# The last weights of an item in the attention denominators: summed by VectorE first, or by TensorE directly, in two of sixteen batch elements

## The chip, the cores and the metric

The kernel runs on one core of a Trainium2 chip. The metric is the device time of one execution in microseconds (us). Everything is in fp32.

## The reference, cut to what matters

The input is x of shape (16, 256, 32, 32): 16 batch elements of 256 channels and 1024 tokens. Each element passes two layers. Layer 0 is an attention with 4 heads of width 64 and a residual. Layer 1 is group norm, an attention with 8 heads of width 32 and a residual, group norm, and an MLP of 256 to 1024 to 256 with gelu and a residual. The change touches layer 1's attention alone:

```python
attn = jnp.einsum('bhnd,bhmd->bhnm', q, k) * scale + phys_bias
attn = jax.nn.softmax(attn, axis=-1)
out = jnp.einsum('bhnm,bhmd->bhnd', attn, v)
out = out.transpose(0, 2, 1, 3).reshape(B, H * W, C)
out = out @ proj_w.T + proj_b
```

A softmax needs, for each query, the sum of the exponentials over all 1024 keys. The kernel does not subtract a maximum first; it watches the range of the denominators, and a second, general pass exists for data that leave it.

## The kernel before

**Stages.** The elements are worked on one after the other. For each one, `first_pass` runs `attention_a` (layer 0), `attention_b` (layer 1) and the MLP, overlapped: the MLP pieces of one element and the projections (q, k, v) of the next one are "pieces" that `run` puts between the steps of an attention. In the first element (b = 0) `attention_b` has only its own seven remaining q, k, v pieces, in steps 0 to 6. In the last one (b = 15) it has these and three MLP pieces, in steps 7, 10 and 13; the other four MLP pieces follow after the stage. The elements between have more pieces to fill with, the next element's projections among them.

**One step of `attention_b`.** Its work is cut into four items (t, c): a half of the queries (t, 512 of them) and four of the eight heads (c). Each item is cut into four units of two key blocks (kb = 0, 2, 4, 6, of 128 keys each), so there are 16 units and 16 steps, counted from 0 here. Step n does this, in program order:

1. `scores(u)`: 16 matmuls into PSUM (s_b, L502; the profile has two records for each fp32 matmul), then five exponentials on ScalarE (L517) into four tiles of weights e_b, each 128 x 1024 in fp32. The scores of one unit use all eight PSUM banks: the banks b0 and b1 and three double tiles.
2. `add` of the unit's first weight tile: a VectorE addition (L533) into one of the item's two running sums es_b. In the item's first unit the first two tiles start the sums.
3. `weigh` of the unit before: 8 matmuls of weights and values into acc_b in bank b0 (L554), which are added to the result res_b, on VectorE (L567), or copied by ScalarE in the item's first unit (L565).
4. `add` of the three other weight tiles.
5. A tick of `later`, and the step's piece, if it has one.

**Denominators.** When an item's last unit has been weighed, `normalise` is put off to the tick behind it. It runs four matmuls of 128 x 32 (den_b, L576, in bank b1), one for each head, of the two running sums against columns that hold exp(bias). Then `denominators` has ScalarE copy den_b (L328), sends it through a DMA into another layout (sp_b, L333), and after some ticks inverts it (L337), writes it to DRAM (row_b, L338), reads it back as four broadcasts (rd_b, L343), and after some ticks more VectorE scales the result by it (L601). The two counts are 1 and 1 for the first three items, 3 and 5 for the fourth, except in the last element, where the fourth item's reciprocal is taken on VectorE directly from PSUM (L586) and the scaling follows at once. The scaling of an item with c = 1 schedules the output projection j of its half of the queries one tick later; the one of the fourth item is handed to the next attention in all but the last element.

**Order.** `later` is a list of functions with a count of ticks. The order on each engine is fixed when the program is built: a planner takes the instructions in the order of the program, but may put a ready instruction ahead of one that is still waiting by its own estimates. `tc.keep_in_program_order` holds some VectorE instructions (additions after the first of a unit, the reciprocal, the scaling) to the order written. Weight tiles e_b have 8 buffers, the sums es_b 4, the inverted denominators rd_b one.

Of the kernel before, what the change touches and what calls it, by code (L numbers as in the profile page):

```python
# [235 lines left out]
def first_pass(ctx, tc, x, out, k):  # L236
    nc = tc.nc
    B, C, S = x.shape
    CC, SB, NT = C // P, S // P, S // TB
    HC = k["w1"].shape[2] // P  # L240
    later = Later()
# [25 lines left out]
    def wide(name, n=None):  # L267
        if n is None:
            n = next(m for m in order if m not in kept)
        use(n)  # L270
        return ps_s.tile([P, 2, TB], F32, tag=f"s{n}", name=name)

    def bank(name, n):
        return ps_a.tile([P, TB], F32, tag=f"b{n}", name=name)
# [203 lines left out]
    def attention_b(b, qT, kT, v, project):  # L478
        key, D = f"b_{b}", D1
        G = P // D  # L480


        items = [(NT - 1, 0)]
        items += [(t, 0) for t in range(NT - 1)] + [(t, 1) for t in range(NT)]
        units = [(i, kb) for i in range(len(items)) for kb in range(0, SB, 2)]
        res, sums = {}, {}

        def scores(i, kb):
            t, c = items[i]
            es = []  # L490
            for m in range(2):
                if m == 0:
                    one, two = (bank(f"s_{key}_{i}_{kb}_{n}", n) for n in range(2))
                    tiles = [None, wide(f"s_{key}_{i}_{kb}_1")]
                    outs = [one, two, tiles[1][:, 0, :], tiles[1][:, 1, :]]
                else:
                    tiles = [wide(f"s_{key}_{i}_{kb + 1}_{n}") for n in range(2)]
                    outs = [tiles[g // 2][:, g % 2, :] for g in range(G)]
                for g in range(G):
                    for h in range(0, P, HALF):  # L500
                        k0 = (kb + m) * P + h
                        nc.tensor.matmul(  # L502
                            outs[g][h : h + HALF, :],
                            kT[g * D : (g + 1) * D, c, k0 : k0 + HALF],
                            qT[g * D : (g + 1) * D, c, t * TB : (t + 1) * TB],
                            start=True,
                            stop=True,
                        )
                for n in range(G // 2):
                    e = work.tile(  # L510
                        [P, 2, TB], F32, tag="e", name=f"e_{key}_{i}_{kb + m}_{n}", bufs=8
                    )
                    for to, s in (
                        [(e, tiles[n])] if tiles[n] is not None
                        else [(e[:, 0, :], one), (e[:, 1, :], two)]
                    ):
                        nc.scalar.activation(to, s, AF.Exp, scale=float(D) ** -0.5)  # L517
                    es.append(e)
            return i, kb, es

        def add(i, kb, es, which):
            if kb == 0 and 0 in which:
                sums[i] = [
                    work.tile([P, 2, TB], F32, tag="es", name=f"es_{key}_{i}_{n}", bufs=4)
                    for n in range(G // 2)
                ]
            for n in which:
                if kb == 0 and n < G // 2:  # L530
                    continue
                d = sums[i][n % 2]
                ins = nc.vector.tensor_add(d, es[n % 2] if kb == 0 else d, es[n])  # L533
                if n:
                    tc.keep_in_program_order(ins)

        def result(t):
            if t < NT - 1 and b == 0:  # L540
                return [
                    work.tile([P, TB], F32, tag="g", name=f"res_{key}_{t}_{c}", bufs=16)
                    for c in range(CC)
                ]
            tag = "res1" if t == NT - 1 else "res" if b < B - 1 else "q0"
            r = act.tile([P, CC, S if tag == "q0" else TB], F32, tag=tag, name=f"res_{key}_{t}")
            return [r[:, c, :TB] for c in range(CC)]

        def weigh(i, kb, es):
            t, c = items[i]  # L550
            acc = bank(f"acc_{key}_{i}_{kb}", 0)
            for m in range(2):
                for g in range(G):
                    nc.tensor.matmul(  # L554
                        acc[g * D : (g + 1) * D, :],
                        v[:, kb + m, c * G + g],
                        es[2 * m + g // 2][:, g % 2, :],
                        start=(m == 0),
                        stop=(m == 1),
                    )  # L560
            if t not in res:
                res[t] = result(t)
            r = res[t][c]
            if kb == 0:
                nc.scalar.copy(r, acc)  # L565
            else:
                nc.vector.tensor_add(r, r, acc)  # L567
            if kb == SB - 2:
                later.after(1, lambda: normalise(i, r, i == len(items) - 1))

        def normalise(i, r, last):
            t, c = items[i]
            at_end = last and b == B - 1
            den = bank(f"den_{key}_{i}", 1)
            for g in range(G):
                nc.tensor.matmul(  # L576
                    den[g * D : (g + 1) * D, :],
                    k["eones"][:, c * G + g],
                    sums[i][g // 2][:, g % 2, :],
                    start=True,  # L580
                    stop=True,
                )
            full = work.tile([P, TB], F32, tag="full", name=f"rd_{key}_{i}", bufs=1)
            if at_end:

                nc.vector.reciprocal(full, den)  # L586
                scale(i, r, last, full)
                for tot, what in ((dsum, den), (isum, full)):
                    part = small.tile([P, 1], F32, tag="part", name="part")
                    nc.vector.tensor_reduce(part, what, AX.X, ALU.add)  # L590
                    nc.gpsimd.tensor_add(tot[:, :1], tot[:, :1], part)
                return
            denominators(
                f"{key}_{i}", den, full, full,
                (3, 5) if last else (1, 1),
                lambda full: scale(i, r, last, full),
            )

        def scale(i, r, last, full):
            t, c = items[i]  # L600
            tc.keep_in_program_order(nc.vector.tensor_mul(r, r, full))  # L601
            if c == CC - 1:
                issue = project(t, res[t])
                if last and b + 1 < B:
                    handed.append(issue)
                else:
                    later.after(1, issue)

        cols[0] = D
        pending = None  # L610
        for u in units:
            now = scores(*u)
            add(*now, (0,))
            if not pending:

                yield
                add(*now, (1, 2, 3))
                pending = now
                continue
            weigh(*pending)  # L620
            add(*now, (1, 2, 3))
            pending = now
            yield
        weigh(*pending)
        yield
        cols[0] = P
# [193 lines left out]
    def attention_1(b, qkv_tiles, xb, norm):  # L820
        q, kk, v = qkv_tiles
        stats = small.tile([P, CC, NT, 6], F32, tag="st1", name=f"st1_{b}", bufs=2)

        def project(t, res):
            return out_proj(
                f"j{b}", k["wpj"],
                lambda kc: res[kc],
                k["pjb"], xb, t, stats, (lambda: norm(stats)) if t == NT - 1 else None,
            )

        return attention_b(b, q, kk, v, project)
# [144 lines left out]
    start = first_qk[::2] + first_qk[1::2] + first_v  # L976
# [23 lines left out]
    last = NT * CC * SB // 2 - 1  # L1000
    for b in range(B):
        if b + 1 < B:
# [5 lines left out]
                lambda st, b=b, xn=xn: group_norm(  # L1008
                    f"g{b}", xs[b], st, k["g1w"], k["g1b"], "res", xn, 3
                ),  # L1010
# [39 lines left out]
        for m, pieces in enumerate(rest):  # L1050
# [5 lines left out]
                lambda st, b=b, hn=hn: group_norm(  # L1056
                    f"h{b}", xs[b], st, k["g2w"], k["g2b"], "q1", hn,
                    3 if b + 1 < B else 1,
                ),
# [311 lines left out]
```

## Time and profile before

| | us |
|---|---|
| median of 3 runs | 3708.99 |
| lowest and highest | 3707.59, 3709.53 |
| the profiled execution | 3707.96 |
| its span | 3706.2 |
| TensorE busy in the span | 3685.2 |
| VectorE busy | 2498.0 |
| ScalarE busy | 2084.0 |
| `attention_b` of the first element | 122.65 to 215.49 |
| `attention_b` of the last element | 3528.94 to 3628.14 |

PE is TensorE, PEld its weight loads, DVE VectorE, ACT ScalarE, POOL GpSimd and SP the engine that issues most DMAs. A row of a group gives the line of the kernel, the engine, the operation, the tiles out and in and the count, then busy time, mean nanoseconds of one, and the idle time before it with what ended it. A row in order of time gives its start, its length from the first to the last of its instructions, engine, line, operation and tiles, and in brackets the idle time before and its releaser. A row of waits gives who waited for whom, the total, the number of times and the longest. The granted TensorE clock was 0.999 of full speed over the span.

### The profile page before, as it was taken

The page shows a single profiled execution, that of the slowest core. Times are in us where ns is not written, and L with a number is a line of the kernel's source. Part 1 is how long each engine was busy: PE and PEld are TensorE (multiplying, and loading weights), DVE is VectorE, ACT ScalarE, POOL GpSimd, SP SyncE. Part 2 cuts the span into 40 slices and gives each one's busy share as a digit, 9 for nine tenths or more (in the row PEclk, how much of TensorE's full clock was granted, in tenths as well). Part 3 has the DMA queues.
Part 4 walks back from the last instruction along what each step waited for, and adds up shares of the span by engine and source line. Part 5 has one row for each costly group of instructions (what it writes and reads, how often), then busy time and mean ns, then how long its engine had stood idle before and what let it go on. Part 6 is the DMA issues. An engine that isn't in the chain of part 4 may idle for free.

```text
span 3706.2 us, 79254 instructions
## 1 busy us (share of the span) xinstructions
PE 3685.2 (99%) x34349; PEld 1319.4 (36%) x34349; DVE 2498.0 (67%) x3150; ACT 2084.0 (56%) x2704; POOL 102.9 (3%) x251
## 2 busy tenths in 40 slices
PE   9999999999999999999999999999999999999999
PEld 4333343333423334333343333433333333333333
DVE  4685757757576675766757667586675867657675
ACT  4665646555465564655646465564655656556472
POOL 1000000000000000000000000000000000000000
PEclk9999999999999999999999999999999999999999
DMA  2000100000001010010000100001010000000000
GB/s 87 12 14 10 33 13 13 31 10 33 13 13 36 4 33 13 19 30 7 30 13 19 30 7 31 13 19 30 8 36 7 22 27 13 30 7 22 16 8 27
DMA packets 63395, 77.80 MB, mean 21 GB/s; under 512 B 35038, under 2 KB 37854, under 8 KB 63038
## 3 DMA queue, kind: packets, MB, share of 16 engines
q1 hardware_dynamic: 60892, 71.85, 6.4%
q8 instruction: 271, 4.44, 0.5%
q14 instruction: 86, 0.70, 0.1%
q10 hardware_dynamic: 1746, 0.40, 0.1%
q0 software_dynamic: 400, 0.41, 0.1%
HBM read 54.28 MB, written 17.56 MB: 19 GB/s over the span
## 4 chain that ended last, share of the span: by engine, by line
PE 94%; DVE 3%; issue 2%; ACT 1%; DMA 1%; ACTq 0%; SPq 0%; POOL 0%; DVEq 0%
PE s_b L502 12%; PE acc_b L554 12%; PE s_a L368 12%; PE m L849 12%; PE acc_a L389 11%; PE m L314 10%; PE qk_a L314 6%; PE qk_b L314 5%; PE o L314 3%; PE v_a L314 3%; PE j L314 3%; PE v_b L314 2%; PE den_b L576 1%; DVE es_b L533 1%; PE den_a L420 1%
## 5 line engine op out<-in xcount | busy, mean ns | idle before, releaser
L517 ACT ACTIVATE e_b<-s_b 128x1024 f32<-128x1024 f32 (+1 forms) x1280 | 982.7, 865 | 151.0 <-PE s_b L502 151.0
L533 DVE TENSOR_TENSOR es_b<-es_b,e_b 128x1024 f32<-128x1024 f32 x768 | 899.5, 1219 | 217.2 <-ACT e_b L517 217.1
L376 ACT ACTIVATE e_a<-s_a 128x1024 f32<-128x1024 f32 x512 | 520.8, 1024 | 360.4 <-PE s_a L368 348.1
L502 PE MATMUL s_b<-q,k 32*64 32x512 f32 x8192 | 527.2, 601 | 9.8 <-DVE v L768 7.1
L368 PE MATMUL s_a<-q,k 64*64 64x512 f32 x4096 | 532.6, 593 | 1.1
L389 PE MATMUL acc_a<-e_a,v 64*64 64x512 f32 x4096 | 528.5, 589 | 0.0
L401 DVE TENSOR_TENSOR es_a<-es_a,e_a 128x1024 f32<-128x1024 f32 x384 | 469.4, 1222 | 75.9 <-ACT e_a L376 60.4
L554 PE MATMUL acc_b<-e_b,v 128*32 128x512 f32 x4096 | 492.1, 598 | 0.0
L849 PE MATMUL m<-gn_h,w 128*128 128x512 f32 x1024 | 452.9, 596 | 0.4 <-DVE gn_h L723 0.4
L314 PE MATMUL m<-g,w2s 128*32 128x512 f32 (+1 forms) x3320 | 404.2, 592 | 0.0
L857 ACT ACTIVATE g<-m,m1b 128x512 f32<-128x512 f32 x256 | 175.9, 687 | 339.3 <-PE m L849 339.3
L866 DVE TENSOR_TENSOR g<-g,g 128x512 f32<-128x512 f32 x320 | 209.3, 686 | 147.7 <-ACT g L857 147.4
L502 PEld LDWEIGHTS s_b<-q,k 32*64 32x64 f32 x8192 | 166.3, 130 | 337.3 <-issue 124.6
L849 PEld LDWEIGHTS m<-gn_h,w 128*128 128x128 f32 x1024 | 191.0, 190 | 236.7 <-issue 235.2
L389 PEld LDWEIGHTS acc_a<-e_a,v 64*64 64x64 f32 x4096 | 161.9, 133 | 277.5 <-issue 235.8
L368 PEld LDWEIGHTS s_a<-q,k 64*64 64x64 f32 x4096 | 152.6, 133 | 278.1 <-issue 207.9
L554 PEld LDWEIGHTS acc_b<-e_b,v 128*32 128x32 f32 x4096 | 108.5, 109 | 357.5 <-ACT e_b L517 194.7
L314 PE MATMUL qk_a<-x,wp 128*32 128x512 f32 (+1 forms) x1856 | 233.7, 592 | 0.4 <-ACT k L747 0.4
L314 PE MATMUL qk_b<-gn_g,wq 128*32 128x512 f32 (+1 forms) x1280 | 234.0, 592 | 0.0
L567 DVE TENSOR_TENSOR res_b<-res_b,acc_b 128x512 f32<-128x512 f32 x192 | 131.8, 687 | 143.7 <-PE acc_b L554 143.7
L314 PEld LDWEIGHTS m<-g,w2s 128*32 128x32 f32 (+1 forms) x3320 | 121.5, 112 | 262.2 <-issue 235.8
L768 DVE TENSOR_TENSOR v<-v_b,eones 128x512 f32<-128x512 f32 x64 | 44.1, 689 | 166.0 <-PE v_b L314 166.0
(131 smaller groups left out, 2371.8 us busy)
## 6 DMA issues: line engine op xcount, KB each, us to landing
d_a<-row_a SPq DMA_DIRECT2D x64, 256.0 KB
rd_b<-row_b SPq DMA_DIRECT2D x252, 64.0 KB
out_dram<-x SPq DMA_DIRECT2D x63, 256.0 KB
x<-in_x_dram SPq DMA_DIRECT2D x30, 512.0 KB
x<-in_x_dram SPq DMA_DIRECT2D x4, 256.0 KB
w<-in_L_conv_mlp_w_dram SPq DMA_DIRECT2D x1, 1024.0 KB
w2s<-in_L_conv_mlp_w_dram SPq DMA_DIRECT2D x4, 256.0 KB
sp_b<-rd_b SPq DMA_DIRECT2D x63, 8.0 KB
```

The source lines that it names most:

```text
L314: nc.tensor.matmul(o[sl], w[:, sl], r, **flags)
L368: nc.tensor.matmul(s[h : h + HALF, g, :], kT[g * D : (g + 1) * D, c, kb * P + h : kb * P + h + HALF], qT[g * D : (g + 1) * D, c, t * TB : ...
L376: nc.scalar.activation(e, s, AF.Exp, scale=float(D) ** -0.5)
L389: nc.tensor.matmul(accs[i][h][g * D : (g + 1) * D, :], v[h * HALF : (h + 1) * HALF, kb, c * 2 + g], e[h * HALF : (h + 1) * HALF, g, :], st ...
L401: nc.vector.tensor_add(sums[i], held[i] if kb == 1 else sums[i], e)
L502: nc.tensor.matmul(outs[g][h : h + HALF, :], kT[g * D : (g + 1) * D, c, k0 : k0 + HALF], qT[g * D : (g + 1) * D, c, t * TB : (t + 1) * TB] ...
L517: nc.scalar.activation(to, s, AF.Exp, scale=float(D) ** -0.5)
L533: ins = nc.vector.tensor_add(d, es[n % 2] if kb == 0 else d, es[n])
L554: nc.tensor.matmul(acc[g * D : (g + 1) * D, :], v[:, kb + m, c * G + g], es[2 * m + g // 2][:, g % 2, :], start=(m == 0), stop=(m == 1),)
L849: nc.tensor.matmul(ps, k["w1"][:, cc, hc * P : (hc + 1) * P], hn[0][:, cc, t * TB : (t + 1) * TB], start=(cc == 0), stop=(cc == CC - 1),)
L857: nc.scalar.activation(g, ps, AF.Gelu, bias=k["m1b"][:, hc : hc + 1])
L866: (nc.vector.tensor_add if plus else nc.vector.tensor_sub)(d, d, gs[(*what, i)])
```

## The change

In `attention_b` of the first and the last element, the four weight tiles of an item's last unit are no longer added to the running sums. The denominators' matmuls take the two sums and these four tiles, in three accumulated rounds of four matmuls in place of one round. In these elements `normalise` is also called at once in `weigh`, behind the last unit's weighted sums, and not from the tick behind that step; what it schedules with counts of ticks then counts from there. The other fourteen elements keep the old form.

```diff
+        direct = b in (0, B - 1)
...
         def add(i, kb, es, which):
+            if direct and kb == SB - 2:
+                return
...
             if kb == SB - 2:
-                later.after(1, lambda: normalise(i, r, i == len(items) - 1))
-
-        def normalise(i, r, last):
+                last = i == len(items) - 1
+                if direct:
+                    normalise(i, r, last, sums[i] + es)
+                else:
+                    later.after(1, lambda: normalise(i, r, last, sums[i]))
+
+        def normalise(i, r, last, parts):
             t, c = items[i]
             at_end = last and b == B - 1
             den = bank(f"den_{key}_{i}", 1)
-            for g in range(G):
-                nc.tensor.matmul(
-                    den[g * D : (g + 1) * D, :],
-                    k["eones"][:, c * G + g],
-                    sums[i][g // 2][:, g % 2, :],
-                    start=True,
-                    stop=True,
-                )
+            for m in range(0, len(parts), G // 2):
+                for g in range(G):
+                    nc.tensor.matmul(
+                        den[g * D : (g + 1) * D, :],
+                        k["eones"][:, c * G + g],
+                        parts[m + g // 2][:, g % 2, :],
+                        start=(m == 0),
+                        stop=(m + G // 2 == len(parts)),
+                    )
```

Here G is 4 (heads of an item), D is 32, SB is 8 (key blocks) and B is 16.

## The prediction

> **What bounds the kernel now.** I read the page first (share of each engine, then the chain that ended last), then the two stretches that the diff touches, the second attention of the first and of the last element, by their busy time, their waits and the rows in order of time.
>
> ```profile
> span 3706.2 us, 79254 instructions
> ...
> PE 3685.2 (99%) x34349; PEld 1319.4 (36%) x34349; DVE 2498.0 (67%) x3150; ACT 2084.0 (56%) x2704; POOL 102.9 (3%) x251
> ...
> PE 94%; DVE 3%; issue 2%; ACT 1%; DMA 1%; ACTq 0%; SPq 0%; POOL 0%; DVEq 0%
> ...
> L533 DVE TENSOR_TENSOR es_b<-es_b,e_b 128x1024 f32<-128x1024 f32 x768 | 899.5, 1219 | 217.2 <-ACT e_b L517 217.1
> ```
>
> TensorE carries 94% of the chain, so a microsecond of new PE work anywhere counts unless PE would have stood idle there. Busy time of the two stretches (first row: first element; second: last):
>
> ```profile
> 122.65:215.49 92.84, 90.16 (x994) 26.30 (x993) 77.56 (x79) 67.39 (x91) 3.02 (x6) 1.00 0.04 11
> 3528.94:3628.14 99.20, 96.73 (x1089) 29.06 (x1088) 85.74 (x93) 69.51 (x95) 2.09 (x6) 1.00 0.05 13
> ```
>
> Columns: length, then PE, PEld, DVE, ACT, POOL. PE looks 97% busy, but matmuls overlap, so I counted records at the spacing at which groups follow each other. A group of 16 acc_b records takes 1.74 us before the next one starts (149.08 to 150.82), 8 den_b records 0.86:
>
> ```profile
> 150.82 1.04 PE L576 MATMUL den_b<-es_b,eones 128*32 128x512 f32 x8
> ...
> 151.68 1.90 PE L314 MATMUL qk_b<-gn_g,wq 128*32 128x512 f32 x16
> ```
>
> The first element has 16 units of 3.44 us (32 s_b, 16 acc_b), 7 pieces of 1.72, four denominators of 0.86 and one j of 3.43: 73.9 us of work in 92.8. PE really idles 19 us there, and by the same count 15 us in the last element. DVE idles 15 and 13. So which idle is DVE's fault? Waits in the first stretch:
>
> ```profile
> PEld s_b L502 <- DVE res_b L567: 7.5, 8, 1.8
> DVE res_b L567 <- PE acc_b L554: 7.3, 8, 1.9
> ```
>
> PE waits for the L567 addition, which frees bank 0, but DVE has mostly been waiting for PE first. The loop is: scores, acc, addition, next scores; its 0.69 us addition is the idle, not DVE's load. Steps 7 to 12 (a step is one unit) show both kinds:
>
> ```profile
> 171.28 1.92 PE L554 MATMUL acc_b<-e_b,v 128*32 128x512 f32 x16
> 173.02 1.04 PE L576 MATMUL den_b<-es_b,eones 128*32 128x512 f32 x8
> 173.27 0.69 DVE L567 TENSOR_TENSOR res_b<-res_b,acc_b 128x512 f32<-128x512 f32 x1 [0.54 <-PE acc_b L554]
> 174.01 2.82 PE L502 MATMUL s_b<-q,k 32*64 32x512 f32 x32
> 174.18 0.63 ACT L328 COPY rd_b<-den_b 128x512 f32<-128x512 f32 x1
> ...
> 186.40 1.92 PE L554 MATMUL acc_b<-e_b,v 128*32 128x512 f32 x16
> ...
> 188.37 1.22 DVE L533 TENSOR_TENSOR es_b<-es_b,e_b 128x1024 f32<-128x1024 f32 x1
> 189.50 0.68 DVE L567 TENSOR_TENSOR res_b<-res_b,acc_b 128x512 f32<-128x512 f32 x1
> ```
>
> At 173 us the den_b group already covers the addition (scores at 174.01, 0.13 us after it). At 189.50 DVE is late: acc_b ended at 188.32, and an addition of the kind to be removed stood in front.
>
> [...]
>
> **The change, part by part.**
> (a) Added: each item's denominator gets three rounds of four matmuls for one. Two extra rounds are 16 records, 1.72 us at 0.86 per 8; eight items (four in each of two elements) make 13.8 us. They stand right behind acc_b, before the next scores. The only idle there is 0.13 us where no piece follows, since the first round and the addition fill it; with a piece behind it, none. All 13.8 is on the path (bounds 12 to 14).
> (b) Removed: four additions an item, 32 in all, 37 us of DVE. Only what PE loses to DVE comes back. First element: step 7 (L567 at 168.64, acc_b over at 168.30) 0.3; step 11 1.2; the last den_b, which waits for the sums, takes 1.41 instead of 1.04, 0.4. Together 1.9. Last element: step 8 (den_b over at 3582.46, scores at 3583.29) 0.7; step 14 0.2; last den_b 0.4. Together 1.3. After it, from 3628.14 to 3647.24, PE has 40 full records of 0.43 us and little else, 17.5 us in 19.1; freed of the additions DVE reaches the reciprocal (L586, 3630.12) sooner relative to den_b, and I take 1.1 of the 1.6 (bounds 0.5 and 1.6). Sum of (b): 4.3 (bounds 3 and 6).
> (c) The step. The den_b matmuls were issued in the tick behind the same acc_b, so they hardly move. What moves is what counts ticks from them: the ACT copy stays, but the reciprocal, POOL's two additions, the store to row and the four loads of rd_b on SP's queue, and the scaling come one step earlier in DVE's and SP's order, in three items of each element; the first element's fourth item shifts too, inside the next stage, where PE has other work. After the copy that ends at 174.81, sp_b is there at 176.87 (2.06 us), after which 5.0 to 6.1 us pass from reciprocal to rd_b (181.19 to 186.19; 160.29 to 166.36). Behind the waiting reciprocal stand the next unit's es_b additions: copy over at 176.53 with two more rounds, reciprocal done at 178.83, exponentials ready at 178.34, so 0.5 us late, which nobody feels. The scaling can start at 183.6 to 184.7, where DVE gets to it at 183.5; then one addition, then L567, due at 185.5 and done 0 to 1.1 us late. PE waits for that: 0.5 in each of two items of the first element, 1.0. Where a piece fills PE (all of the last element, and the first item) it is covered; without the piece it would cost the same 0.5. In step 9 of the last element bank 1 now waits for the copy, 0.6.
> (d) The projection j of the first half moves from step 15 to step 14. There it covers the 1 us of waiting for L567, and uncovers 1.3 us of waiting for exponentials in step 15; its wide tile must be drained by DVE before the last scores. I take 0 (bounds -1 and +2 each). POOL and SP stand idle around this; a late landing would show at the scaling only.
> Sum: 13.8 - 4.3 + 1.6 = +11.1. The profiled execution took 3707.96 us (span 3706.2 and 1.8 around it), so it would take 3719. The median of the runs shown is 1.0 above it: 3720.
>
> **The rivals.**
> 1. **DVE is the bound in these stretches** (faster). From about 3610 to 3640 us it is 100% busy. If every step were as long as DVE's own work, 37 us would go, against 13.8 of PE: -23, 3686. It decides where L567 is late in most steps; against it, DVE waited 7.3 us for acc_b in the first stretch, and I find lateness in few steps. 0.13.
> 2. **The rounds fall into idle PE time** (same). 34 us of idle exist. The orders on the engines are fixed by a planner at build, which does run ready work ahead (an m group stands between halves of j at 3632.54). If it ran half of the 16 rounds into waits, 6.9 us would go: +4, 3713. Against: the last rounds need e_b and bank 1, free only just before acc_b. 0.11. That the change did not do what it says would end here too: the same places, no more than 4 us.
> 3. **The earlier round trip stalls DVE** (slower by more). If in six items reciprocal and scaling hold up L567 by 1.5 us each, that is 8 more than I took: 3728. For it: the copy, two DMA legs and the scaling take 8 us, more than a bare step of 4.63 (scores at 179.86 to 184.49). 0.10.
> The forecast itself has 0.66.
>
> **How the numbers follow.** The terms' bounds give 3714.5 to 3724.5 for the forecast's own case. A measurement here can tell about 0.2%, 7.4 us, from no change; 3716.4 lies inside that case, so of its 0.66 I put 0.60 on slower and 0.06 on same. With the rivals: slower 0.60 + 0.10 = 0.70; same 0.06 + 0.11 = 0.17; faster 0.13. The range to leave no more than 2 in 10 out is 3705 to 3728: it takes in rival 2, most of rival 3 and none of rival 1's full gain.
>
> **What would show it.** den_b in these elements: 12 matmuls, 24 records for 8, about 2.6 us from its start to the next group's. es_b: 32 fewer additions, DVE about 37 us less busy, total PE records up by 128. L567 right behind acc_b in step 11, rd_b's scaling one step earlier. The first stretch should grow by 6.0 us (6.9 - 1.9 + 1.0), the last by 5.1 (6.9 - 2.4 + 0.6), taken to the first m of L849. If they do not grow though den_b does, the idle time was not where I put it; if steps shorten where I find DVE on time, rival 1 is right.

## The result, and the profile after

The changed kernel takes 3731.72 us (median of 4 runs, 3730.02 to 3732.86) against 3709.26 for the kernel before: 22.5 us more, a ratio of 1.0061 (95% interval 1.0043 to 1.0078). The direction was forecast, the size was not: 3720 was predicted, and 3731.72 lies above the range.

The page of the changed kernel, the lines that answer to those of before:

```profile
span 3729.0 us, 79497 instructions
...
PE 3705.5 (99%) x34501; PEld 1324.4 (36%) x34501; DVE 2462.8 (66%) x3118; ACT 2085.1 (56%) x2704; POOL 107.0 (3%) x251
...
PE 95%; DVE 2%; issue 1%; ACT 1%; DMA 1%; SPq 0%; DVEq 0%; ACTq 0%
...
L538 DVE TENSOR_TENSOR es_b<-es_b,e_b 128x1024 f32<-128x1024 f32 x736 | 861.5, 1218 | 219.7 <-ACT e_b L520 219.5
```

VectorE has the 32 additions less and is 35 us less busy (37 was forecast); the span is 22.8 us longer. TensorE has 152 records more: the 128 of the new rounds, as forecast, and 24 because the very last projection j now runs as 32 records of 128 x 32 in place of 8 of 128 x 128. The stretches can be measured by marks that both traces have. From the first scores s_b to the first s_a of the next attention, the first element's stretch went from 92.84 to 102.99 us (+10.1). From the first s_b of the last element to the first m of its MLP (L849 before, L859 now), 118.30 became 131.36 (+13.1). Together they are 23.2 us, the whole difference of the spans.

The step with the new rounds looks as forecast. In order of time, the first element, step 8:

```profile
174.79 1.04 PE L586 MATMUL den_b<-es_b,eones 128*32 128x512 f32 x8
...
175.65 1.90 PE L586 MATMUL den_b<-e_b,eones 128*32 128x512 f32 x16
...
177.48 2.74 PE L505 MATMUL s_b<-q,k 32*64 32x512 f32 x32
```

The denominator takes 2.69 us (174.79 to 177.48) where it took 0.99 in the kernel before (173.02 to 174.01): 1.7 more, with nothing to hide it. Up to the scores of step 14 the first element is only 4.6 us behind (205.59 less 122.92, against 200.72 less 122.65). The other 5.5 us come in the last two steps (the fourth denominator's two rounds, 1.7 us by the spacing above, are among them). There the kernel before had the projection j in step 15, behind the last scores, and VectorE emptied j's tile (L641) while nobody waited for it:

```profile
204.48 2.85 PE L502 MATMUL s_b<-q,k 32*64 32x512 f32 x32
...
209.00 3.62 PE L314 MATMUL j<-res_b,wpj 128*32 128x512 f32 x32
212.43 1.90 PE L554 MATMUL acc_b<-e_b,v 128*32 128x512 f32 x16
...
214.37 1.41 DVE L641 SCALAR_TENSOR_TENSOR x<-j,pjb,x 128x512 f32<-128x512 f32 x2
```

The changed kernel, steps 14 and 15:

```profile
208.78 0.69 DVE L611 TENSOR_TENSOR res_b<-res_b,rd_b 128x512 f32<-128x512 f32 x1 [1.69 <-DMA rd_b<-row_b]
209.23 3.62 PE L314 MATMUL j<-res_b,wpj 128*32 128x512 f32 x32
...
211.12 3.49 DVE L538 TENSOR_TENSOR es_b<-es_b,e_b 128x1024 f32<-128x1024 f32 x3
212.78 1.95 PE L505 MATMUL s_b<-q,k 32*64 32x512 f32 x24
...
214.53 1.40 DVE L651 SCALAR_TENSOR_TENSOR x<-j,pjb,x 128x512 f32<-128x512 f32 x2
...
216.07 1.17 PE L505 MATMUL s_b<-q,k 32*64 32x512 f32 x8 [1.35 <-DVE x L651]
217.17 3.48 PE L559 MATMUL acc_b<-e_b,v 128*32 128x512 f32 x16
```

The projection j now stands ahead of the last unit's scores and holds one of the three double tiles of PSUM. VectorE empties it (L651), but three es_b additions stand in front of that, until 214.5. So 24 records of s_b run and the last 8, which need this tile, start at 216.07: TensorE issues nothing for about 2 us (24 records at 0.43 us for 8, their spacing in the trace, end at about 214.1; the row counts the last record's modelled end and so shows 1.35 as idle). Then acc_b takes 3.48 us where it takes 1.92 elsewhere. The busy time of PE by microsecond shows why; "granted clock" is the share of its full clock that TensorE was given. The columns are the stretch, its length, PE busy (with the number of instructions), the granted clock, the DMA share and GB/s:

```profile
216.00:217.00 1.00, 0.93 (x8) 0.97 0.06 16
217.00:218.00 1.00, 1.00 (x8) 0.50 0.00 0
218.00:219.00 1.00, 1.00 (x12) 0.50 0.00 0
219.00:220.00 1.00, 1.00 (x12) 0.50 0.00 0
220.00:221.00 1.00, 1.00 (x6) 0.82 0.00 0
```

About 2 us of idle time came before, and then TensorE ran at half its clock (0.50) for 3.41 us, from 216.95 to 220.36, which loses 1.7 us (0.5 + 0.5 + 0.5 + 0.2).

The last element has the same wait in step 15 (1.49 us, and 1.7 us of half clock behind it) and a second one. A row of the first, then the second as a row of waits (who waited for whom, total, times, longest):

```profile
3638.72 1.09 PE L505 MATMUL s_b<-q,k 32*64 32x512 f32 x8 [1.49 <-DVE x L651]
...
PE m L314 <- DVE x L651: 2.3, 1, 2.3
```

Here the projection of the second half of the queries came a tick earlier too. It used the stage's narrow form with one double tile, and the MLP's m waited until VectorE had emptied it. Another half clock of 3.4 us starts within this wait, at 3657.58.

### The profile page after: what moved, and what is told of

The parts are those of the page before. It is cut to its first block, busy times and chain, and to the rows that moved or that the text cites. A ratio compares the mean times of both kernels' runs of the same rounds, so it can differ in the third digit from the quotient of the medians.

```text
span 3729.0 us, 79497 instructions
## 1 busy us (share of the span) xinstructions
PE 3705.5 (99%) x34501; PEld 1324.4 (36%) x34501; DVE 2462.8 (66%) x3118; ACT 2085.1 (56%) x2704; POOL 107.0 (3%) x251
## 4 chain that ended last, share of the span: by engine, by line
PE 95%; DVE 2%; issue 1%; ACT 1%; DMA 1%; SPq 0%; DVEq 0%; ACTq 0%
PE s_b L505 13%; PE acc_b L559 12%; PE m L859 12%; PE s_a L368 12%; PE acc_a L389 11%; PE m L314 10%; PE qk_a L314 6%; PE qk_b L314 5%; PE o L314 3%; PE v_a L314 3%; PE j L314 3%; PE v_b L314 2%; PE den_b L586 2%; DVE es_b L538 1%; PE den_a L420 1%
## 5 line engine op out<-in xcount | busy, mean ns | idle before, releaser
L538 DVE TENSOR_TENSOR es_b<-es_b,e_b 128x1024 f32<-128x1024 f32 x736 | 861.5, 1218 | 219.7 <-ACT e_b L520 219.5
L376 ACT ACTIVATE e_a<-s_a 128x1024 f32<-128x1024 f32 x512 | 521.0, 1024 | 360.3 <-PE s_a L368 348.5
L859 PE MATMUL m<-gn_h,w 128*128 128x512 f32 x1024 | 452.8, 596 | 0.0
L859 PEld LDWEIGHTS m<-gn_h,w 128*128 128x128 f32 x1024 | 191.0, 190 | 235.9 <-issue 235.9
L572 DVE TENSOR_TENSOR res_b<-res_b,acc_b 128x512 f32<-128x512 f32 x192 | 131.6, 686 | 178.8 <-PE acc_b L559 178.8
```

The source lines that it names most:

```text
L376: nc.scalar.activation(e, s, AF.Exp, scale=float(D) ** -0.5)
L859: nc.tensor.matmul(ps, k["w1"][:, cc, hc * P : (hc + 1) * P], hn[0][:, cc, t * TB : (t + 1) * TB], start=(cc == 0), stop=(cc == CC - 1),)
```

## The experiments

**Theory T:** the loss beyond the forecast comes from the earlier step, and in it from the projection j, which takes a PSUM tile whose emptying is queued behind additions. **Rival R:** the rounds on TensorE cost more than their matmuls. **Rival S:** the earlier round trip of the reciprocal costs it. Differences are medians against the kernel before, timed beside each. An edit is shown against the changed kernel, and against the kernel before for the last two.

| kernel | median, us | before, us | difference | ratio (95% interval) | half clocks | span at full clock |
|---|---|---|---|---|---|---|
| the change | 3731.72 | 3709.26 | +22.5 | 1.0061 (1.0043 to 1.0078) | 3 | +17.7 |
| old_step | 3718.87 | 3708.96 | +9.9 | 1.0028 (1.0017 to 1.0038) | 1 | +8.7 |
| early_only | 3723.39 | 3708.96 | +14.4 | 1.0039 (1.0025 to 1.0053) | 5 | +12.4 |
| rounds_only | 3720.71 | 3708.96 | +11.8 | 1.0032 (1.0019 to 1.0044) | 1 | +10.9 |
| adds_out | 3705.09 | 3708.96 | -3.9 | 0.9990 (0.9984 to 0.9997) | 0 | -3.9 |
| j_held | 3720.14 | 3709.10 | +11.0 | 1.0032 (1.0020 to 1.0044) | 1 | +11.9 |
| j_end_held | 3724.59 | 3709.10 | +15.5 | 1.0043 (1.0029 to 1.0057) | 3 | +14.4 |
| first_only | 3717.58 | 3709.10 | +8.5 | 1.0025 (1.0016 to 1.0034) | 0 | +8.6 |
| last_only | 3719.14 | 3709.10 | +10.0 | 1.0031 (1.0019 to 1.0043) | 2 | +9.9 |
| pool_half | 3718.36 | 3707.64 | +10.7 | 1.0026 (1.0016 to 1.0036) | 4 | +5.9 |
| v_first | 3702.40 | 3707.64 | -5.2 | 0.9984 (0.9977 to 0.9991) | 0 | -5.6 |

The last two columns are of the one profiled execution of each kernel: how often TensorE's clock fell to half while it had work, and the span less 1.7 us for each of these (1.68 to 1.71 by the granted clock), against the 3706.2 us of the kernel before, whose profile has none. This "span at full clock" is an estimate, good to about 1 us (for old_step the two stretches taken alone give 9.6 in place of 8.7). It matters because, by the same estimate, a half clock more or less in the usual execution moves a median by 1.7 us. The kernel before falls into two groups in the 26 executions of the last two rows: 15 took 3706.67 to 3707.74 us and 11 took 3709.31 to 3710.94. The mean granted clock of an execution reads 1.0 for 11 of the first group and for none of the second (0.998 and 0.999). The groups' medians are 2.1 us apart, of which one half clock would make 1.7; this is an estimate, since no profile of the second group was kept.

**old_step: the change without the step.**

```diff
-                if direct:
-                    normalise(i, r, last, sums[i] + es)
-                else:
-                    later.after(1, lambda: normalise(i, r, last, sums[i]))
+                parts = sums[i] + es if direct else sums[i]
+                later.after(1, lambda: normalise(i, r, last, parts))
```

> The sums are left to TensorE as in the change (three rounds, four additions fewer an item), but normalise stays in the tick behind the step. Theory T (the loss beyond the forecast is the earlier step, which brings the projection j one step ahead): the forecast's terms (a) and (b) alone, 13.8 - 4.3 = +9.5 us, so 3718 to 3720, with j in step 15 again and no wait of s_b for L651. Rival R (the rounds cost more than their 0.86 us each, through the planner's order): +20 us or more, 3729 or above.

+9.9 us. Theory T's number; rival R is out. No s_b waits for the emptying of j. The first element's stretch is 97.82 us, +4.98.

**early_only: the step alone** (the additions and the single round kept).

```diff
-            if direct and kb == SB - 2:
-                return
...
-                    normalise(i, r, last, sums[i] + es)
+                    normalise(i, r, last, sums[i])
```

> The four additions and the single round are kept; only normalise is called at once, so that all that counts ticks from it is one step early. Theory T: +11 to +15 us, since the double tile of j must be drained by a VectorE that is fuller than in the change, 3720 to 3724. Rival R: 0 to +2 us.

+14.4 us, within theory T's numbers. TensorE's three waits for the emptying of j (L649 in this kernel) are 1.89, 2.64 and 2.23 us, two of them longer than in the change, as a fuller VectorE would make them. By the medians the step alone costs a little more than the rounds alone (11.8, next), but the intervals overlap.

**rounds_only: TensorE's part alone.**

```diff
-            if direct and kb == SB - 2:
-                return
...
+                parts = sums[i] * 3 if direct else sums[i]
+                later.after(1, lambda: normalise(i, r, last, parts))
...
-                        start=(m == 0),
-                        stop=(m + G // 2 == len(parts)),
+                        start=True,
+                        stop=True,
```

> The additions and the old step are kept, and the one round over the two sums is issued three times over (each overwrites the one before), so TensorE has the change's extra 64 matmuls and nothing else changes. Both take the price of the rounds from this: at 0.86 us for 8 records all on the path +13.8 us, 3722 to 3724. Theory T says 12 to 15; rival R says 20 or more.

+11.8 us, a little under the 12 to 15 expected and far from 20. In the profile the first element's stretch grows by 6.65 us, close to the full price of 6.9, and the last one's by 4.94 at full clock. So the 2 us that the rounds do not cost are hidden in idle time of the last element.

**adds_out: VectorE's part alone.**

```diff
-                if direct:
-                    normalise(i, r, last, sums[i] + es)
-                else:
-                    later.after(1, lambda: normalise(i, r, last, sums[i]))
+                later.after(1, lambda: normalise(i, r, last, sums[i]))
```

> The four additions of an item's last unit are left out in the two elements and the old step and the single round are kept, so the denominators there lack the last unit's weights. This measures what VectorE's freed 37 us give: the forecast said -4.3 us (bounds -3 to -6), 3703 to 3706. The rival in which VectorE is the bound says -20 us or more.

-3.9 us. 37 us of VectorE time are worth 4: it is not the bound in these stretches. By the medians the parts make 11.8 - 3.9 = 7.9 and both together cost 9.9, a difference that lies within the intervals. In the first element's profiles they add: 6.65 - 1.69 = 4.96, against 4.98. In the last one's, at full clock, they do not: 4.94 - 2.02 = 2.92, against 4.63. What overlaps there was not traced.

**j_held: the change, with j back in its old step.** The reciprocal and the scaling stay early.

```diff
                 else:
-                    later.after(1, issue)
+                    later.after(2 if direct else 1, issue)
```

> The change as it is, with one edit: the projection j waits two ticks behind the scaling, not one, in the two elements, so it stands where it stood before, while the reciprocal, its DMAs and the scaling stay a step early. Theory T (the loss beyond the forecast is the early j): the 9.9 us of the old step with three rounds, and 1 to 2 for the earlier round trip, so 3719 to 3722, no wait of s_b for L651 and no half clock in step 15. Rival S (the earlier round trip of the reciprocal costs it): 3729 or above.

+11.0 us: this one line takes back 11.5 of the 22.5 us. Rival S is out; the earlier round trip costs 11.0 less 9.9 of old_step, about 1, by the medians. At full clock the profiles put it at about 3 (11.9 less 8.7): TensorE waits 0.80 and 0.73 us for a late L572 in the first element (scores at 190.56 and 212.85) and 1.01 in the last (3632.10), which it does not do in old_step. The end of the first element in order of time:

```profile
212.71 3.49 DVE L538 TENSOR_TENSOR es_b<-es_b,e_b 128x1024 f32<-128x1024 f32 x3
...
216.49 3.62 PE L314 MATMUL j<-res_b,wpj 128*32 128x512 f32 x32
...
219.93 1.90 PE L559 MATMUL acc_b<-e_b,v 128*32 128x512 f32 x16
220.18 1.41 DVE L651 SCALAR_TENSOR_TENSOR x<-j,pjb,x 128x512 f32<-128x512 f32 x2 [2.75 <-PE j L314]
...
221.64 1.04 PE L586 MATMUL den_b<-es_b,eones 128*32 128x512 f32 x8
```

j stands behind the last scores again, acc_b follows at once, and L651 empties the tile while nobody waits for it: VectorE waited for j (2.75), not TensorE for VectorE.

**j_end_held: only the very last projection held.**

```diff
-                    later.after(1, issue)
+                    later.after(2 if last else 1, issue)
```

> The change, with only the very last projection (second half of the queries of the last element) held one tick longer; the j of the first half stays early in both elements. Theory T: the wait of the MLP's m for L651 (2.3 us) and the half clock behind it go, the ones in step 15 stay: 4 to 5 us less than the change, 3726 to 3729. Rival S: no difference, 3731.

+15.5 us, 7.0 less than the change and lower than expected. The profiled executions differ by less: spans of 3725.7 and 3729.0. By the medians the last projection has 7.0 of j's 11.5 us, and the first half's j in both elements the other 4.5 (15.5 - 11.0); the executions vary by 3.5 us, so this split is rough. The half clock behind the last wait is gone, but this execution has another one in step 3 of the last element. At full clock the last projection has 3.3 us (17.7 - 14.4), of which 2.31 are its wait, and the first half's two j 2.5 (14.4 - 11.9).

**first_only and last_only: the change in one of the two elements.**

```diff
-        direct = b in (0, B - 1)
+        direct = b == 0
```

```diff
-        direct = b in (0, B - 1)
+        direct = b == B - 1
```

> The change in the first element alone. By the stretch in the change's profile (102.99 us against 92.84) +10 us, 3718 to 3720; had the loss come from elsewhere in the order of the whole program, it would not split so.

> The change in the last element alone. By the stretch up to the first m of L859 in the change's profile (131.36 us against 118.30) +12 to +13 us, 3720 to 3723.

+8.5 and +10.0 us, both below what the change's profile had suggested and below the ranges expected. The profile of first_only has the wait, but not the half clock:

```profile
216.31 1.09 PE L505 MATMUL s_b<-q,k 32*64 32x512 f32 x8 [1.47 <-DVE x L651]
217.32 1.92 PE L559 MATMUL acc_b<-e_b,v 128*32 128x512 f32 x16
```

So the wait comes with the order of the instructions (1.35 us in the change, 1.47 here), and a half clock came behind it in the one profiled execution and not in the other. It came elsewhere too: in the profile of j_held it follows the idle time of step 3 (a wait of 1.21 us), which the kernel before has as well (1.22). PE busy by two microseconds, first element:

```profile
144.00:146.00 2.00, 2.00 (x12) 0.57 0.00 0
146.00:148.00 2.00, 2.00 (x16) 0.57 0.00 0
```

The two single-element effects sum to 18.5, not 22.5. At full clock the sum closes: 8.6 + 9.9 = 18.5, against 17.7 for the change. The three profiles have 0, 2 and 3 half clocks, one more in the change than in the two others together, which is 1.7 us by the estimate; that half clocks make up the other 4 us of the medians was not shown, since a profile shows one execution.

**pool_half: two of the four additions on GpSimd**, in the kernel before.

```diff
+                if b in (0, B - 1) and kb == SB - 2 and n % 2:
+                    nc.gpsimd.tensor_add(d, d, es[n])
+                    continue
                 ins = nc.vector.tensor_add(d, es[n % 2] if kb == 0 else d, es[n])
```

> Not the change, but what its parts point to: leaving the last unit's additions off VectorE gave about 4 us, and three rounds on TensorE cost about 12. Here the kernel before has, in the two elements, two of the four additions of each item's last unit on GpSimd (those of the second sum), which is idle 97% of the span; the step and the single round are as before. If GpSimd keeps up (den_b does not wait for it): 1 to 3 us below the kernel before, 3706 to 3708. If an addition of this size takes GpSimd over 2.5 us, den_b waits for it in eight places: 5 to 15 us above.

+10.7 us. The instructions on es_b in the first element, count, then nanoseconds of one (least, median, most):

```profile
L536 DVE TENSOR_TENSOR es_b<-es_b,e_b x40: 1209/1219/3404, 130.1 to 220.2; 128x1024 f32<-128x1024 f32 x40
...
L534 POOL TENSOR_TENSOR es_b<-es_b,e_b x8: 2372/3220/3261, 143.2 to 218.7; 128x1024 f32<-128x1024 f32 x8
```

An addition took 3.22 us at the median on GpSimd and 1.22 on VectorE, and some VectorE additions took up to 3.4 us in this kernel. The freed time was more than given back, though not by the way expected: TensorE's matmuls waited for GpSimd's sum in den_b only twice (0.27 and 0.88 us), and longer for a late L570 (3.06 us, behind a VectorE addition of 3.36, and 2.15 us). Four half clocks fell into the profiled execution, so at full clock the loss is only 5.9 us.

**v_first: v_b emptied ahead of the additions**, in the kernel before. The idle of step 3, seen in the profiles of all the kernels above, is a wait for the multiplication that empties v_b, behind three additions (rows of the kernel before):

```profile
138.44 3.49 DVE L533 TENSOR_TENSOR es_b<-es_b,e_b 128x1024 f32<-128x1024 f32 x3
141.85 0.69 DVE L768 TENSOR_TENSOR v<-v_b,eones 128x512 f32<-128x512 f32 x1
142.59 1.09 PE L502 MATMUL s_b<-q,k 32*64 32x512 f32 x8 [1.22 <-DVE v L768]
143.61 1.92 PE L554 MATMUL acc_b<-e_b,v 128*32 128x512 f32 x16
```

The edit is in the kernel before, for the first item of both elements:

```diff
             weigh(*pending)
+            if b in (0, B - 1) and now[0] == 0:
+                yield
+                add(*now, (1, 2, 3))
+                pending = now
+                continue
...
-                nc.vector.tensor_mul(
+                ins = nc.vector.tensor_mul(
                     d, ps, v_scale.unsqueeze(1).to_broadcast([P, 2, C // D, D])
                 )
+                if key in ("b0", f"b{B - 1}"):
+                    tc.keep_in_program_order(ins)
```

> The kernel before, with the largest idle of TensorE in these stretches taken on: in the first item of both elements the step's tick and piece come ahead of the three later additions, and the multiplication that empties v_b from PSUM (L768 of the kernel before) is held to program order, so it no longer stands behind three additions. In steps 2 and 3 the scores waited for it 1.0 and 1.9 us. Theory: 2 to 5 us less over both elements, 3704 to 3707, and no half clock after step 3. Rival: VectorE now waits for v_b with its additions behind it, so L567 comes late instead: no gain, or 1 to 3 us more.

-5.2 us, 3702.40, slightly more than the 2 to 5 expected. The same place in its trace (step 3 of the first element begins with the last row):

```profile
138.45 0.68 DVE L567 TENSOR_TENSOR res_b<-res_b,acc_b 128x512 f32<-128x512 f32 x1
139.04 0.68 DVE L773 TENSOR_TENSOR v<-v_b,eones 128x512 f32<-128x512 f32 x1
139.18 1.98 PE L502 MATMUL s_b<-q,k 32*64 32x512 f32 x32 [0.46 <-DVE res_b L567]
```

v_b is emptied before the additions, and all 32 records run without a break. Each element's stretch is 2.64 us shorter (92.84 to 90.20, 118.30 to 115.66). VectorE does the same work in another order, and by the medians that is worth no less than the 37 us taken off it in adds_out (the intervals overlap). The 18 executions lie within 1.2 us (3701.70 to 3702.91); the two groups of the kernel before are gone. Half clocks behind step 3 in some executions of the kernel before would fit that; its one profile has none, so it was not shown.

## Why the prediction was right or wrong

- **What bounds the kernel** was right. TensorE's own work and the waits in its loop set the time. Rival 1 (VectorE is the bound) is refuted by adds_out, rival 2 (half of the rounds fall into idle time) by rounds_only, where 2 us of 13.8 do.
- **(a) the rounds** at +13.8: alone they measure +11.8, just under the lower bound of 12. **(b) the additions** at -4.3: alone -3.9. The 37 us for 32 additions are 1.16 us each, but they follow each other at about 1.14 (three in 3.49), so 36 us were to go from VectorE. The two together were to cost 9.5 and cost 9.9 in old_step; in the first element's profile 4.98, where 6.9 - 1.9 = 5.0 was worked out.
- **(c) the earlier round trip** at +1.6: j_held less old_step is 1.1 by the medians and about 3 at full clock. The late scaling in two places of the first element can be seen in the change (L611 waits 1.61 us for rd_b at 186.37 and 1.69 at 208.78); in j_held it costs TensorE 0.80 and 0.73 us, where 0.5 each was forecast, and 1.01 in the last element, which was taken as covered. Rival 3, with 8 us more, was wrong.
- **(d) the projection** was the step that failed. It was put at 0, with bounds of -1 and +2 for each, and measures 11.5 us (the change less j_held), of which about 6 at full clock. Three things were wrong in it. That VectorE must empty j's tile before the last scores was written down, but not priced: the time at which VectorE comes to it had to be read off the queue, where es_b's three additions of 3.49 us stand ahead. That gives the waits of 1.35 and 1.49 us. Second, only the first half's j was looked at; the second half's in the last element moved too, ahead of the stage's end, which gives the wait of 2.31 us. Third, a wait was priced at its own length; in the profiled execution each of the three had a half clock with it (from 216.95, 3640.52 and 3657.58) that lost about 1.7 more, about 5 in all.
- At full clock the sum comes out like this: 8.7 for (a) and (b), where 9.5 was forecast, 3.2 for (c), where 1.6 was, and 5.8 for (d), where 0 was: +17.7 in place of +11.1. The waits with L651 as releaser sum to 5.15; the forecast gain and loss of (d) in steps 14 and 15 (the covered L567, the exposed exponentials) were not isolated. The rest of the +22.5, about 4.8 us, is about what three half clocks lose by the estimate of 1.7 each.
- The range held the sum of the priced terms but not an unpriced stall: (d) decided the size. The bounds of the terms, with (c) at 1.6, sum to 3714.6 to 3725.6, not to the 3724.5 noted as the upper end; the result lies above both.

## What to carry to other kernels

When a step is moved, follow everything that counts from it to the last buffer that it takes, and ask at what time the engine that must free this buffer comes to it in its own queue: here one line about a projection decided half of the loss (11.5 of 22.5 us). Ask also which waits the time of an engine that is not the bound causes: here some 36 us taken off VectorE gave 3.9, and another order of its queue gave 5.2. Price a wait with what came behind it: in the change's profile TensorE's waits of 1.35, 1.49 and 2.31 us each had a half clock with them that lost about 1.7 more. When half clocks come and go between executions, compare the profiles with these taken off before a difference of 2 us is explained.

## What the runs showed of the hardware

- TensorE's granted clock fell to 0.50 for 3.41 us after an idle stretch of about 2 us in the change (216.95 to 220.36, the wait of 1.35 us), and did not after a like one in first_only (1.47 us). In the twelve profiles the wait in step 3, which v_first does not have, was followed by a half clock in 9 of 22 cases, TensorE's waits for the emptying of j in 9 of 11.
- The half clocks did not start at a fixed delay. In the change one began 0.9 us after TensorE's work resumed (216.95, work from 216.07), one 1.8 after (3640.52, from 3638.72), and one 0.3 before (3657.58, from 3657.88). What sets the start was not shown.
- In pool_half a 128 x 1024 fp32 addition took 3.22 us at the median on GpSimd (2.37 at the least); VectorE's additions of this size, 1.22 us at the median, took up to 3.40 us in that kernel.
